# Second self-attention of a two-block transformer kernel: the order of scores, projections, values and row sums

## The chip, the cores and the metric

The kernel runs on one core of one Trainium2 chip. The metric is the device time of one execution in microseconds; lower is better. All arithmetic is in float32.

## What is computed

The input is x of shape 8 x 512 x 256 (batches, rows, width) with a condition vector per batch and a short context. Two blocks follow each other; each has a self-attention, a cross-attention to the context and a feed-forward part, all with residuals. The change lies in the self-attention of the second block. Cut to it, the reference is:

```python
attn_in = _adaln(x, cond, ln1_w, ln1_b, g1_w, g1_b, b1_w, b1_b)   # layer norm, scaled and shifted per batch
q = heads(attn_in @ wq); k, v = heads of (attn_in @ wkv)          # 16 heads of 64
q = _rope(q, sq, cq); k = _rope(k, sk, ck)                        # rotary, on even and odd channels
sim = jnp.einsum('bhnd,bhmd->bhnm', q, k) * 64 ** (-0.5)
a = jax.nn.softmax(sim, axis=-1)
o = jnp.einsum('bhnm,bhmd->bhnd', a, v)
x = unheads(o) @ sa_wo + sa_bo + x
```

The softmax is computed without subtracting a maximum: exponentials of the scores, their products with v, and sums of the exponentials, by which the products are divided at the end.

## The kernel before, in words

The kernel goes through three stages: the first block, the second block's self-attention (the part with the pool "ph4", lines 953 to 1155), and the second block's cross-attention and feed-forward part. In the second, `tc.manual_schedule` is set for PE, DVE, ACT and POOL: each of these engines executes in the order in which the code issues. Only the DMA queue of SP is ordered by the framework.

**The work of a batch.** `batch4(b)` makes the functions for one batch of 512 rows. Heads are handled in NG = 4 groups g of four heads. Keys lie in NT = 4 tiles kt of 128 rows. A step i = 16 b + 4 g + kt is one pair (g, kt), 128 steps in all.

- `score(g, kt)` (line 1003) makes 8 matmuls with 32 contraction rows each, four beside each other in the array, into two tiles of two PSUM banks (`bank_s`, two buffers, so one step fills both). Two exponentials on ACT (L1012) turn them into probabilities p. The pool has six p buffers, two to a step.
- `value(g, kt)` (line 1014) multiplies p with v into one bank O and one bank D, accumulated over kt: 4 matmuls with 64 output rows, two beside each other. At kt = 0 it adds the p of kt 0 and 1 on POOL (L1027, two of them); at kt = 2 it adds the p of kt 2 and 3 to that on DVE (L1031, four). At kt = 3 ACT copies O and D to oT (L1035).
- `sums(g)` (line 1041) is 4 matmuls with ones that add sm over the partitions, into an X bank; ACT copies it (L1047), SP sends it through DRAM back as a dense tile rec.
- `inverse(g)` (line 1057) takes the reciprocal on DVE (L1059), sends it to DRAM, and fetches it back spread over the partitions (rb, L1071, four DMAs).
- `scaled(g)` (line 1074) multiplies oT with rb on POOL (L1077, two).
- `queries(g)` and `keys(g)` (through `turned`, line 983) are a projection into two X banks: even and odd channels, 2 matmuls each. DVE makes four rotary products (L991, L992), POOL adds them up (L994, L995). `values(half, ts)` (line 973) is a projection of the same PE time into two X banks, which ACT copies (L981).
- `out_tiles(qp)` is half of the output projection into one X bank; DVE adds it to x (L453).
- `rows_` is the layer norm of the next batch: on DVE statistics (L183, L184), an add (L174), the normalized rows z (L187, four), with a power on POOL in between (L175); then POOL adds the bias row to x (L437). `turn` transposes z on PE (L416) into two X banks, from which ACT writes hT (L417).

There are two X banks in this stage, used in turn: `bank_x()` gives the one that was taken the longer ago, and its first matmul waits until that bank has been read.

**The slots.** Two steps make a slot; slot m holds the steps 2m and 2m + 1, and a batch begins at slot base = 8 b. `last(slot, fn)` puts a job into the list of a slot. With r = m - base, and b' the next batch, the lists in the middle of the stage are:

| r | jobs in order (before) | kt of the slot |
|---|---|---|
| 0 | values of half 1 (t 0, 1); keys(1); inverse(3) of the batch before | 0, 1 |
| 1 | values of half 1 (t 2, 3); queries(2); scaled(3) of the batch before | 2, 3 |
| 2 | out_tiles(0) of the batch before; keys(2); inverse(0) | 0, 1 |
| 3 | out_tiles(1) of the batch before; queries(3); rows_ of b'; scaled(0) | 2, 3 |
| 4 | keys(3); inverse(1) | 0, 1 |
| 5 | turn of b'; queries(0) of b'; scaled(1) | 2, 3 |
| 6 | values of half 0 of b' (t 0, 1); keys(0) of b'; inverse(2) | 0, 1 |
| 7 | values of half 0 of b' (t 2, 3); queries(1) of b'; scaled(2) | 2, 3 |

The function `slots()` (line 1124) issues, slot by slot: the scores of 2m, the values of 2m - 1, the sums of the group that has just ended (`mid`, in even slots), the scores of 2m + 1, the values of 2m, and then the jobs of the slot. So on PE a slot runs scores, values, (sums), scores, values, projections. The last batch has no next one: its slots 61 and 63 have no job for PE, and slot 62 only the sums.

## Time and profile before

| what | value |
|---|---|
| median of three runs | 2453.35 us (2447.49 to 2454.86) |
| the profiled execution | 2448.82 us, its span 2446.9 us |
| granted TensorE clock, mean | 0.997 |
| stage of the second self-attention (first to last exponential) | 883.5 to 1837 us |
| L1012, exponential | 1022 ns, 256 of them |
| L1031, sum of p on DVE | 1532 ns mean, 128 of them |
| L1027, sum of p on POOL | 2354 ns mean, 64 of them |
| L994 and L995, rotary sums on POOL | 1272 ns mean for the queries, 1480 for the keys |
| L1077, scaling on POOL | 1307 ns mean, 63 of them |
| L991 and L992, rotary product on DVE | 692 and 680 ns |

The profile is one execution. Busy time of an engine is the time in which at least one of its instructions runs. A float32 matmul appears as two records of PE, and records overlap each other, so the start of one group to the start of the next is the better measure of what a group takes on PE. The line of a wait names the instruction on the other engine that came last before the waiting one went on. All PE instructions of matmuls are recorded under the helper's line L109, so groups are told apart by the tiles that they read and write.

### The profile page before, as it was taken

How to read it: one execution, taken by the hardware profiler on the slowest of the kernel's cores; microseconds unless marked ns; L12 is line 12 of the kernel's file. 1: busy time of each engine (PE TensorE's matmuls, PEld its weight loads, DVE VectorE, ACT ScalarE, POOL GpSimd, SP SyncE). 2: the span in 40 equal slices, each digit the busy share in tenths (PEclk: the TensorE clock that was granted, in tenths of full speed). 3: DMA queues.
4: the chain of work that ended last, by engine and by line, in shares of the span. 5: the costliest groups of instructions: out<-in, count | busy, mean ns of one | idle time of the engine just before them, and what ended most of it. 6: DMA issues, size and time to landing. Idle time of an engine off the chain costs nothing.

```text
span 2446.9 us, 28449 instructions
## 1 busy us (share of the span) xinstructions
PE 2408.0 (98%) x10964; PEld 1157.3 (47%) x10964; DVE 1058.9 (43%) x2083; ACT 878.5 (36%) x1118; POOL 858.5 (35%) x538
## 2 busy tenths in 40 slices
PE   9999999999998999999999999999999999999999
PEld 4333443444435643444444444434345555566665
DVE  5544435434434434343434343434334766651210
ACT  4565545545452123333333333333332221222221
POOL 3443222222301026343434343434333444531110
PEclk9999999999999999999999999999999999999999
DMA  5120000000001000000000000000123222210000
GB/s 181 45 93 7 16 20 8 17 11 12 13 11 64 27 1 23 18 19 19 19 18 19 18 19 19 19 18 19 36 61 96 68 67 67 64 55 27 22 18 23
DMA packets 84400, 84.07 MB, mean 34 GB/s; under 512 B 42544, under 2 KB 58784, under 8 KB 84256
## 3 DMA queue, kind: packets, MB, share of 16 engines
q1 hardware_dynamic: 83352, 81.09, 10.6%
q8 instruction: 88, 1.44, 0.2%
q10 hardware_dynamic: 904, 1.07, 0.1%
q14 instruction: 56, 0.46, 0.1%
HBM read 72.09 MB, written 10.04 MB: 34 GB/s over the span
## 4 chain that ended last, share of the span: by engine, by line
PE 92%; DVE 3%; issue 1%; ACT 1%; DMA 1%; POOL 1%; SPq 0%; POOLq 0%; DVEq 0%; ACTq 0%
PE ps_X L109 38%; PE ps_S L109 23%; PE ps_O L109 14%; PE ps_D L109 14%; PE ps_X L416 1%; DVE t L836 1%; DMA rec<-rec 1%; DMA rb<-rec 1%; POOL p L1252 1%; ACT p L574 0%; PE ps_X L554 0%; PE ps_X L596 0%; PE ps_D L416 0%; DVE t L833 0%; ACT hT L417 0%
## 5 line engine op out<-in xcount | busy, mean ns | idle before, releaser
L109 PE MATMUL ps_S<-q,k 32*128 32x512 f32 (+1 forms) x3072 | 429.1, 625 | 7.3 <-ACT p L574 3.1
L1012 ACT ACTIVATE p<-ps_S 128x1024 f32<-128x1024 f32 x256 | 248.1, 1022 | 522.1 <-PE ps_S L109 522.1
L574 ACT ACTIVATE p<-ps_S 128x1024 f32<-128x1024 f32 x256 | 248.2, 1021 | 232.1 <-PE ps_S L109 230.7
L109 PEld LDWEIGHTS ps_S<-q,k 32*128 32x128 f32 (+1 forms) x3072 | 160.5, 184 | 233.1 <-issue 137.5
L991 DVE TENSOR_TENSOR t<-ps_X,rope_c 128x512 f32<-128x512 f32 x126 | 87.2, 692 | 349.9 <-PE ps_X L109 349.9
L1031 DVE TENSOR_TENSOR sm<-sm,p 128x1024 f32<-128x1024 f32 x128 | 190.6, 1532 | 59.2 <-ACT p L1012 59.2
L994 POOL TENSOR_TENSOR q<-t 128x512 f32<-128x512 f32 x32 | 40.8, 1276 | 406.6 <-DVE t L992 406.6
L175 POOL TENSOR_TENSOR rstd<-rstd,mhalf 128x4 f32<-128x4 f32 x49 | 51.0, 1042 | 326.8 <-DVE rstd L174 325.2
L1027 POOL TENSOR_TENSOR sm<-p 128x1024 f32<-128x1024 f32 x64 | 149.3, 2354 | 38.0 <-ACT p L1012 38.0
L109 PE MATMUL ps_X<-hT,w 128*128 128x512 f32 x344 | 160.5, 601 | 1.3 <-ACT hT L417 0.9
L837 POOL TENSOR_TENSOR q<-t,t 128x512 f32<-128x512 f32 x72 | 95.1, 1321 | 176.4 <-DVE t L836 172.4
L109 PE MATMUL ps_O<-p,h 128*32 128x512 f32 x1024 | 139.4, 614 | 1.6 <-ACT oT L587 1.6
L109 PE MATMUL ps_O<-p,v 128*64 128x512 f32 x512 | 138.0, 617 | 0.0
L109 PE MATMUL ps_D<-p,v 128*64 128x512 f32 x512 | 131.6, 592 | 0.0
L453 DVE TENSOR_TENSOR x<-ps_X,x 128x512 f32<-128x512 f32 x27 | 18.7, 692 | 239.4 <-PE ps_X L109 239.4
L109 PE MATMUL ps_X<-hT,w_sa_wq 128*128 128x512 f32 x256 | 115.9, 595 | 3.0 <-ACT hT L417 3.0
L109 PE MATMUL ps_X<-w_sa_wv,hT 128*128 128x512 f32 x256 | 118.0, 604 | 0.0
L109 PE MATMUL ps_X<-w_sa_wo,oT 128*128 128x256 f32 x512 | 114.5, 382 | 0.1
L545 POOL TENSOR_TENSOR var<-var,mhalf 128x32 f32<-128x32 f32 (+1 forms) x17 | 87.3, 5135 | 75.2 <-ACT t L773 41.7
L109 PE MATMUL ps_X<-hT,w_sa_wk 128*128 128x512 f32 x248 | 112.4, 596 | 0.0
L109 PE MATMUL ps_S<-hT,w_ff_w 128*128 128x512 f32 x256 | 111.3, 592 | 0.0
L109 PEld LDWEIGHTS ps_X<-w_sa_wo,oT 128*128 128x128 f32 x512 | 96.0, 190 | 24.2 <-issue 11.4
(282 smaller groups left out, 3537.0 us busy)
## 6 DMA issues: line engine op xcount, KB each, us to landing
rb<-rec SPq DMA_DIRECT2D x128, 128.0 KB
rb<-rec_d SPq DMA_DIRECT2D x124, 128.0 KB
rb<-rec SPq DMA_DIRECT2D x16, 256.0 KB
out_dram<-x SPq DMA_DIRECT2D x15, 256.0 KB
x<-in_x_dram SPq DMA_DIRECT2D x7, 512.0 KB
bc<-modd SPq DMA_DIRECT2D x7, 384.0 KB
gate<-modd SPq DMA_DIRECT2D x16, 128.0 KB
k_d<-q SPq DMA_DIRECT2D x8, 256.0 KB
```

What stands on the lines that cost most here:

```text
L109: nc.tensor.matmul(o, lhsT, rhs, start=start, stop=stop)
L175: nc.gpsimd.tensor_tensor(r[:, :n], r[:, :n], mhalf[:, :n], ALU.pow)
L416: nc.tensor.transpose(ps[:, t * P : (t + 1) * P], z[:, t, k * P : (k + 1) * P], ident)
L545: nc.gpsimd.tensor_tensor(var, var, half, ALU.pow)
L574: nc.scalar.activation(pr[u], pss[u], AF.Exp, scale=HD0 ** -0.5)
L836: nc.vector.tensor_tensor(t2[d], ps[src], sn[src].to_broadcast([64, *shape[1:]]), ALU.mult)
L837: nc.gpsimd.tensor_tensor(dst, t1, t2, ALU.add)
L991: nc.vector.tensor_tensor(c, ps, rope_c, ALU.mult)
L994: nc.gpsimd.tensor_tensor(r[0], ec, os, ALU.subtract)
L1012: nc.scalar.activation(pr, pss[u], AF.Exp, scale=HD1 ** -0.5)
L1027: nc.gpsimd.tensor_tensor(sm, s["p", g, 0, u], s["p", g, 1, u], ALU.add)
L1031: nc.vector.tensor_tensor(s["sm", g, u], s["sm", g, u], s["p", g, t, u], ALU.add)
```

## The change

In each slot the order becomes: the scores of 2m + 1, the first job of the slot, the sums (in even slots), the other jobs, the scores of 2m + 2, the values of 2m and of 2m + 1, and then `inverse`. So a slot runs scores, projection, (sums), projection, scores, values, values on PE. `inverse` leaves the list of jobs for a list of its own, `after`. The sums on POOL and DVE (L1027, L1031) belong to `value`, and so they are issued behind the slot's jobs. The slots begin at m = -1, where the first batch's projections are issued ahead of the first scores, and end with m = 63. The functions of a step and of a job are not changed.

```diff
-        steps, mid = {}, {}
+        steps, mid, after = {}, {}, {}
...
                 n = base + 2 * g + 2
                 mid[n] = lambda g=g, f=sums: f(g)
-                last(n, lambda g=g, f=inverse: f(g))
+                after[n] = [lambda g=g, f=inverse: f(g)]
                 last(n + 1, lambda g=g, f=scaled: f(g))
...
             n = B * NG * NT
-            for i in range(-2, n + 1):
-                if 0 <= i < n:
+            for m in range(-1, n // 2):
+
+                i = 2 * m + 1
+                if i >= 0:
                     todo[i // 16][0](i % 16 // NT, i % NT)
-                if 1 <= i <= n:
-                    todo[(i - 1) // 16][1]((i - 1) % 16 // NT, (i - 1) % NT)
-                if i % 2 == 0 and i // 2 in mid:
-                    mid[i // 2]()
-                if i % 2:
-                    for fn in steps.get(i // 2, []):
-                        fn()
+                jobs = steps.get(m, [])[:]
+                if m in mid:
+                    jobs.insert(1, mid[m])
+                for fn in jobs:
+                    fn()
+                if i + 1 < n:
+                    todo[(i + 1) // 16][0]((i + 1) % 16 // NT, (i + 1) % NT)
+                for k in (i - 1, i):
+                    if k >= 0:
+                        todo[k // 16][1](k % 16 // NT, k % NT)
+                for fn in after.get(m, []):
+                    fn()
                 if i == n - 5:
                     cross_weights()
```

## The prediction

> **What bounds the kernel now.** I read the page's busy times first, then the groups by shape, then the timeline of one batch in the second self-attention (883 to 1841 us).

> ```profile
> span 2446.9 us, 28449 instructions
> PE 2408.0 (98%) x10964; PEld 1157.3 (47%) x10964; DVE 1058.9 (43%) x2083; ACT 878.5 (36%) x1118; POOL 858.5 (35%) x538
> ```

> PE is busy 98%, so whatever adds idle time to PE adds it to the end. In the stage the cycle of eight slots repeats each 119 us almost to the hundredth, so I read prices from start to start of PE groups. Three stretches of the timeline (start, duration, engine, line, output and inputs, count, idle time before):

> ```profile
> 1302.40 3.60 PE L109 MATMUL ps_X<-hT,w_sa_wq 128*128 128x512 f32 x8
> ...
> 1305.00 0.68 DVE L992 TENSOR_TENSOR t<-ps_X,rope_s 128x512 f32<-128x512 f32 x1
> 1305.93 2.00 PE L109 MATMUL ps_S<-q,k 32*128 32x512 f32 x16
> ...
> 1311.23 1.38 DVE L187 TENSOR_SCALAR z<-x,mv,rstd 128x256 f32<-128x256 f32 x4 [1.14 <-POOL rstd L175]
> ...
> 1312.69 2.37 POOL L437 TENSOR_TENSOR x<-x,rows 128x1024 f32<-128x1024 f32 x1 [1.50 <-DVE z L187]
> ```

> The projection ends at 1305.93. Behind it DVE still has half the rotary products and the whole norm of the next batch; z ends at 1312.61, 6.68 us after the projection. Only then can POOL add the bias row.

> ```profile
> 1320.18 1.94 ACT L1012 ACTIVATE p<-ps_S 128x1024 f32<-128x1024 f32 x2 [5.49 <-PE ps_S L109]
> 1320.99 1.03 PE L109 MATMUL ps_D<-p,v 128*64 128x512 f32 x4
> ...
> 1321.31 7.48 DVE L1031 TENSOR_TENSOR sm<-sm,p 128x1024 f32<-128x1024 f32 x4 [1.33 <-ACT p L1012]
> 1321.95 2.21 PE L109 MATMUL ps_S<-q,k 32*128 32x512 f32 x16
> 1322.11 2.25 POOL L994 TENSOR_TENSOR k<-t 128x512 f32<-128x512 f32 x1
> 1324.04 1.94 ACT L1012 ACTIVATE p<-ps_S 128x1024 f32<-128x1024 f32 x2 [1.92 <-PE ps_S L109]
> ...
> 1325.96 1.09 PE L416 MATMUL ps_X<-ident,z 128*128 128x128 f32 x8
> 1326.65 1.45 ACT L417 ACTIVATE hT<-ps_X,b,a 128x512 f32<-128x512 f32 x2 [0.67 <-PE ps_X L416]
> 1327.48 3.70 PE L109 MATMUL ps_X<-hT,w_sa_wq 128*128 128x512 f32 x8 [0.43 <-ACT hT L417]
> ```

> Scores take 1.93 us, but 2.14 (1321.95 to 1324.09) where only one value step stands between two score steps: the exponentials end at 1322.12, after the next scores began. A turn's queries wait 0.43 us for ACT. The four sums (L1031) take 7.48 us because POOL works beside them.

> ```profile
> L1031 DVE TENSOR_TENSOR sm<-sm,p x128: 1209/1224/2298, 899.5 to 1837.8; 128x1024 f32<-128x1024 f32 x128
> ```

> Alone an L1031 takes 1.22 us; beside POOL's rotary sum it takes up to 2.30.

> [...] 1.22 becomes 2.30, near 1.22 plus POOL's 1.27. [...]

> **The change part by part.** I call the slots of a batch r = 0 to 7.

> *Values of two steps together.* A value step alone takes 0.91 + 0.96 = 1.87 us. At the stage's end two stand together already, and the inner groups take 0.86: 0.91 + 0.86 + 0.86 + 0.96 = 3.59 for two instead of 3.74. Gain 63 x 0.15 = 9.5 us.

> *Scores, projections, scores.* 34 score groups follow a value step and take 72.5 us; at 1.93 each they would take 65.6. After the change 3.6 us of values or a projection of 3.5 stand between, so the exponentials (1.94) end in time. Gain 6.9 us. Going from scores straight into a projection never happens in this trace. I take it as costly as from scores into values (both then use all 128 rows): 0. Bounds: free, which removes 0.22 of the scores and 0.10 at the projection's start, 63 x 0.32 = -20 us; or another 0.22 each, +14 us.

> *Sums behind the first projection.* In r = 0, 2, 6 they now split two projections. A 128-row group after a switch costs 0.10 more (3.63 against 3.53), and 0.10 more before one: 0.2 x 21 = 4.2 us. In r = 4 there is one projection, so the sums split nothing: 0 for the switch.

> *The vector queue in r = 3 and 4: the main cost.* Before, the four L1031 of slot r = 3 were queued ahead of that slot's projections. Now value() comes after the jobs, so they stand behind the rotary products and the whole norm, and start at 6.68 us after the projection's end. There they meet POOL's bias row (2.37) and the two scalings (1.28 each), all on SBUF. One after the other: 4 x 1.22 + 2.37 + 2 x 1.28 = 9.8; a contested pair measures 2.3, not 2.5, so I take off 0.2 for each of three: 9.2. They end at 15.9. Behind them in the queue stand the rotary products of keys(3); its even half (1304.39 to 1305.68) takes 1.3, to 17.2. Only then is that X bank free, and sums(1), placed just behind keys(3), takes the next X bank of two, which is that one. With 0.1 for the signal it starts at 17.3. PE is there at 1.93 + 3.59 + 1.93 + 3.63 = 11.1. Stall 6.2 us, in the seven batches with a next one: 43.4 us. Bounds: no contention, 6.68 + 4.9 + 1.4 = 13.0, stall 1.9, 13 us in all; strict alternation, 6.8, 48 us. In the last batch (no norm) the sums end at 1.5 + 4 x 2.3 = 10.7, the rotary half at 12.0, and the stall is 1.0 us.

> *The turn in r = 5.* Before, a value step ran between the scores and the transposes. Now transposes follow at once, and on ACT the copies into hT stand behind two exponentials. From the scores' end: exponentials to 1.9, first copy (half of 1.45 and the latency, 0.8) to 2.7, so the queries start at 2.7 instead of 1.52. Cost 1.2 x 7 = 8.4 us.

> *The end.* In slots 61 and 62 there is no projection left: scores follow scores. At the stage's start such a pair takes 5.94 us instead of 3.86, so 2.1; with sums (1.0) between, 1.1. Cost 3.2 us.

> *Moved at no cost.* inverse() with its reciprocal and five DMAs on SP now comes after the values. In even slots DVE has no L1031, so the reciprocal waits for rec while DVE is empty; behind it stand only the next slot's rotary products, over 8 us off. The rb copies were issued 1321.20 to 1323.58 and used at 1335.21; the sums come 4 to 9 us later than before within the slot, the scaling comes at the end of the next slot's POOL work, so some 10 us remain. If that cover went, scaled() would hold POOL's queue. Probabilities: six buffers are three steps; a step's scores need the buffers two slots' L1031 or L1027 release. POOL's pair (4.7 us, behind 2.5 of rotary sums and 1.5 of DVE) ends 8.7 us after a projection, while the second exponential wants its buffer at 8.5: 0.2 us, hidden by the projection that follows. In r = 0 and 6 the sums want the L1031 at 11.0 us and these end at 10.7: hidden by 0.3 us. If that goes, 15 slots lose some 0.5 us each, 7 us.

> *Sum.* -9.5 - 6.9 + 4.2 + 43.4 + 1.0 + 8.4 + 3.2 = +43.8 us. The profiled execution took 2448.82 us (span 2446.9 and 1.9 around it), giving 2492.6. The median shown is 2453.35, 4.5 us above it, and would give 2497.2. I put the forecast between, at 2494.

> **Rivals.** *Light stall:* POOL's work doesn't slow the sums (its ropes beside PSUM reads show none), so r = 4 loses 1.9 us: 43.8 - 30 = +14, 2464. Against it: a mean of 1532 ns over a median of 1224 (page and row above) means that a quarter or more of the 128 L1031 were slowed to some 2.3 us. *Not slower:* the r = 4 wait doesn't occur at all, sums and rotary half being done by 11.1 us. What is left is 43.8 - 43.4 = +0.4: 2450. It decides from the point where DVE does four L1031 and half a rotation in 4.4 us after z; the rows say 6.2 alone, so the norm would have to be done earlier. For it speaks that the norm has its own inputs, against it the written order. *Worse:* leaving the scores costs 0.22 more and the narrow slots slip as well: 43.8 + 14 + 7, 2515. *The change does nothing:* excluded, since the order of PE is written out by hand and the changed code has the new sequence.

> **How the numbers follow.** Forecast 0.60, with a range of its own from 2478 to 2510 (16 us to either side: the score exit's +14 or most of its -20, and the stall's 48 at the top); light stall 0.18; not slower 0.12; worse 0.10. The range 2462 to 2513 leaves out the not-slower case and half of the worse one, 0.17. About 0.3% (7 us) is what a measurement of this kernel can tell from no change. Faster by more needs the not-slower case and a free exit from the scores: 0.05. Within 0.3%: 0.11. Slower: 0.84.

> **What would show it.** Right: value groups of 0.86 inside a pair; no score group of 2.14; each batch but the last with a PE gap of some 6 us before the sums of r = 4, released by DVE's L992; L1031 in r = 3 starting after L187 and mostly near 2.3; queries after a turn waiting 1.6 instead of 0.43. Wrong: no gap in r = 4, or a projection after scores that takes more or less than 3.63 us.

## The result and the profile after

The changed kernel takes 2475.19 us (median of four runs, 2474.84 to 2479.44) against 2453.04 us before (the three runs above and one more). It is slower by 22 us; the ratio taken over all runs is 1.0098, with a 95% interval of 1.0079 to 1.0118. The forecast was 2494 us with a range of 2462 to 2513. The profiled executions differ by 26.0 us (2474.84 against 2448.82), and all of it lies in the second self-attention: from its first exponential to its last copy of O and D that stage takes 982.1 us instead of 956.2.

The head of the page of the changed kernel:

```profile
span 2472.9 us, 28440 instructions
PE 2404.0 (97%) x10964; PEld 1144.8 (46%) x10964; DVE 1088.0 (44%) x2083; ACT 888.1 (36%) x1118; POOL 959.1 (39%) x538
```

PE has the same instructions and is busy 4 us less, in a span that is 26 us longer. So the matmuls themselves became cheaper, and PE idles more. DVE is busy 29 us longer and POOL 101 us longer with the same work: their instructions now run beside each other more often, and are longer there. The row of L1031 shows it (durations are least, median and greatest, in ns; the median was 1224 before):

```profile
L1031 DVE TENSOR_TENSOR sm<-sm,p x128: 1210/2284/2307, 909.8 to 1863.1; 128x1024 f32<-128x1024 f32 x128
```

The timeline of the changed kernel from r = 3 to r = 5 of one batch (start, duration, engine, line, output and inputs, count, idle time before):

```profile
1313.61 2.00 PE L109 MATMUL ps_S<-q,k 32*128 32x512 f32 x16
...
1318.91 1.38 DVE L187 TENSOR_SCALAR z<-x,mv,rstd 128x256 f32<-128x256 f32 x4 [1.14 <-POOL rstd L175]
1319.12 2.00 PE L109 MATMUL ps_S<-q,k 32*128 32x512 f32 x16
...
1320.21 4.63 DVE L1031 TENSOR_TENSOR sm<-sm,p 128x1024 f32<-128x1024 f32 x4
1320.38 6.68 POOL L437 TENSOR_TENSOR x<-x,rows 128x1024 f32<-128x1024 f32 x1 [1.50 <-DVE z L187]
1321.05 3.70 PE L109 MATMUL ps_X<-hT,w_sa_wk 128*128 128x512 f32 x8
...
1324.75 0.69 DVE L991 TENSOR_TENSOR t<-ps_X,rope_c 128x512 f32<-128x512 f32 x1
...
1326.09 1.06 PE L109 MATMUL ps_X<-sm,ones 128*32 128x512 f32 x8 [1.33 <-DVE t L992]
...
1331.92 4.66 POOL L1027 TENSOR_TENSOR sm<-p 128x1024 f32<-128x1024 f32 x2
...
1334.53 1.09 PE L416 MATMUL ps_X<-ident,z 128*128 128x128 f32 x8
1334.69 1.02 ACT L1012 ACTIVATE p<-ps_S 128x1024 f32<-128x1024 f32 x1 [3.63 <-PE ps_S L109]
1336.62 1.02 ACT L1012 ACTIVATE p<-ps_S 128x1024 f32<-128x1024 f32 x1 [0.91 <-POOL sm L1027]
1337.54 1.44 ACT L417 ACTIVATE hT<-ps_X,b,a 128x512 f32<-128x512 f32 x2
1338.37 1.98 PE L109 MATMUL ps_X<-hT,w_sa_wq 128*128 128x512 f32 x4 [2.75 <-ACT hT L417]
```

Three things are to be seen. First, the sums of r = 4 wait 1.33 us for DVE's rotary product, as forecast in kind, but not 6.2: the four L1031 ran through in 4.63 us, and it was POOL's bias row that took longer (6.68 us instead of 2.37). Second, that put POOL's queue late: L1027 comes late, so the second exponential of r = 5 waits for its buffer until 1336.62, and behind it on ACT the copies into hT. The queries of the turn wait 2.75 us. Third, in some batches the matmuls behind that gap run at half the clock. The two stretches below are the queries of one batch and of another (columns: length, busy time of each engine, then the granted clock, DMA share, GB/s):

```profile
1465.00:1468.00 3.00, 3.00 (x5) 1.12 (x4) 0.00 (x0) 0.00 (x0) 0.00 (x0) 0.50 0.00 0
1338.00:1342.00 4.00, 3.63 (x9) 1.44 (x9) 1.29 (x2) 0.98 (x2) 0.00 (x0) 1.00 0.00 0
```

From starts of groups on PE, the whole difference adds up, next to the forecast's terms:

| term | forecast, us | measured, us |
|---|---|---|
| values in pairs | -9.5 | -9.5 (0.91, 0.86, 0.86, 0.96 in every slot) |
| scores no longer late | -6.9 | -6.9 (all 63 behind values take 1.93) |
| scores straight into a projection | 0 | 0 (1.93; the projection 3.54 where another follows it, 3.63 where not) |
| projections split by the sums | +4.2 | +4.0 |
| wait before the sums of r = 4 | +43.4 + 1.0 | +8.4 in six batches, +3.8 in the first, 0 in the last |
| turn | +8.4 | +15.4 (2.3 in six batches, 1.5 in the first) |
| end of the stage | +3.2 | +3.0 |
| half clock | not foreseen | +6.4 behind three turns, +0.9 in the first batch's sums |
| sum | +43.8 | +25.5 (the stage: +25.9) |

The first batch is another case: in its r = 4 another job stands first in the list, so its sums come ahead of keys(3), straight behind the scores, and wait for L1031 itself: 2.7 us before the first two matmuls and 1.1 before the other two. The 1.1 is read from the kernels below in which the clock stays full there (2.12 us for these sums instead of 1.00); here they take 2.99.

### The profile page after: what moved, and what is told of

Same layout as the page of the kernel before. It is cut to its first block, busy times and chain, and to the rows that moved or that the text cites. A ratio compares the mean times of both kernels' runs of the same rounds, so it can differ in the third digit from the quotient of the medians.

```text
span 2472.9 us, 28440 instructions
## 1 busy us (share of the span) xinstructions
PE 2404.0 (97%) x10964; PEld 1144.8 (46%) x10964; DVE 1088.0 (44%) x2083; ACT 888.1 (36%) x1118; POOL 959.1 (39%) x538
## 4 chain that ended last, share of the span: by engine, by line
PE 85%; DVE 4%; POOL 4%; issue 4%; ACT 2%; DMA 1%; SPq 0%; POOLq 0%; DVEq 0%; ACTq 0%
PE ps_X L109 37%; PE ps_S L109 20%; PE ps_D L109 13%; PE ps_O L109 13%; POOL sm L1027 1%; PE ps_X L416 1%; DVE t L836 1%; DMA rb<-rec 1%; POOL p L1259 1%; ACT p L574 0%; DMA rec<-rec 0%; ACT p L1012 0%; PE ps_X L554 0%; DVE st L183 0%; SPq L1252 0%
## 5 line engine op out<-in xcount | busy, mean ns | idle before, releaser
L109 PE MATMUL ps_S<-q,k 32*128 32x512 f32 (+1 forms) x3072 | 422.8, 622 | 9.3 <-DVE k L558 3.6
L1012 ACT ACTIVATE p<-ps_S 128x1024 f32<-128x1024 f32 x256 | 252.2, 1023 | 492.7 <-PE ps_S L109 471.3
L109 PEld LDWEIGHTS ps_S<-q,k 32*128 32x128 f32 (+1 forms) x3072 | 142.2, 183 | 248.0 <-issue 178.6
L991 DVE TENSOR_TENSOR t<-ps_X,rope_c 128x512 f32<-128x512 f32 x126 | 87.0, 691 | 374.4 <-PE ps_X L109 374.3
L1031 DVE TENSOR_TENSOR sm<-sm,p 128x1024 f32<-128x1024 f32 x128 | 222.7, 1799 | 2.0 <-ACT p L1012 2.0
L994 POOL TENSOR_TENSOR q<-t 128x512 f32<-128x512 f32 x32 | 59.7, 1866 | 306.1 <-DVE t L992 306.1
L175 POOL TENSOR_TENSOR rstd<-rstd,mhalf 128x4 f32<-128x4 f32 x49 | 51.0, 1041 | 327.0 <-DVE rstd L174 325.4
L109 PE MATMUL ps_X<-hT,w 128*128 128x512 f32 x344 | 160.5, 601 | 1.3 <-ACT hT L417 0.9
L1027 POOL TENSOR_TENSOR sm<-p 128x1024 f32<-128x1024 f32 x64 | 149.1, 2353 | 3.4 <-ACT p L1012 3.4
L109 PE MATMUL ps_X<-hT,w_sa_wq 128*128 128x512 f32 x256 | 122.3, 623 | 18.4 <-ACT hT L417 18.4
L109 PE MATMUL ps_O<-p,h 128*32 128x512 f32 x1024 | 137.8, 608 | 1.6 <-ACT oT L587 1.6
L109 PE MATMUL ps_O<-p,v 128*64 128x512 f32 x512 | 134.8, 605 | 0.0
L109 PE MATMUL ps_D<-p,v 128*64 128x512 f32 x512 | 131.6, 592 | 0.0
L1077 POOL TENSOR_TENSOR oT<-oT,rb 128x512 f32<-128x512 f32 x63 | 123.5, 1978 | 18.7 <-DMA rb<-rec_d 18.7
L109 PE MATMUL ps_X<-w_sa_wv,hT 128*128 128x512 f32 x256 | 118.0, 604 | 0.0
L994 POOL TENSOR_TENSOR k<-t 128x512 f32<-128x512 f32 x32 | 40.8, 1274 | 192.3 <-DVE t L992 185.0
L109 PE MATMUL ps_X<-hT,w_sa_wk 128*128 128x512 f32 x248 | 114.7, 605 | 0.0
L109 PE MATMUL ps_X<-w_sa_wo,oT 128*128 128x256 f32 x512 | 114.5, 382 | 0.1
```

The lines of the kernel that those rows point to most:

```text
L109: nc.tensor.matmul(o, lhsT, rhs, start=start, stop=stop)
L175: nc.gpsimd.tensor_tensor(r[:, :n], r[:, :n], mhalf[:, :n], ALU.pow)
L991: nc.vector.tensor_tensor(c, ps, rope_c, ALU.mult)
L994: nc.gpsimd.tensor_tensor(r[0], ec, os, ALU.subtract)
L1012: nc.scalar.activation(pr, pss[u], AF.Exp, scale=HD1 ** -0.5)
L1027: nc.gpsimd.tensor_tensor(sm, s["p", g, 0, u], s["p", g, 1, u], ALU.add)
```

## The experiments

The theory after this reading: gains on PE of 16 us are real; the loss is three waits, and they hang together: the norm ahead of L1031 delays the sums and POOL; late POOL delays the turn; a long idle time of PE is followed by half clock. The rival for the first is that of the forecast, contention of L1031 with the rotary sums and scalings themselves; for the turn, that it waits for two exponentials only; for the clock, that the slow matmuls have another cause than idle time. All times below are medians; before took 2450.1 to 2450.4 us beside them.

**The norm one slot earlier.** It is issued ahead of its slot's projections.

```diff
-                last(base - 5, rows_)
+                if b > 1:
+                    early[base - 6] = rows_
+                else:
+                    last(base - 5, rows_)
...
+                if m in early:
+                    early[m]()
                 jobs = steps.get(m, [])[:]
```

> The changed kernel, with the norm of batches 2 to 7 issued one slot earlier (r = 2, ahead of that slot's projections), so that in r = 3 the four L1031 stand behind the rotary products alone. Theory A (the norm ahead of L1031 is what makes the sums of r = 4 wait, and POOL's late bias row is what makes the exponential behind L1027, and with it the turn, late): the 1.4 us before the sums of r = 4 vanish in six batches (-8.4 us), the turn's transposes and wait shrink from 3.84 to about 2.7 us in those six (-6.8 us), and PE idle of 2.75 us is gone, so with it the half-clock stretches behind the turn (-6.4 us): 2475 - 21 = 2454 us. Rival B (the turn waits for two exponentials only, whatever POOL does, as I predicted, and the surplus of 1.1 us is something else): only the 8.4 us go, 2467 us. Rival C (the wait of r = 4 comes from contention of L1031 with the rotary sums and the scalings and not from the norm): no gain at r = 4, about 2475 us.

Measured: 2458.33 us (2453.76 to 2463.73), ratio to before 1.0032 (1.0020 to 1.0044). In one of the six batches:

```profile
1313.37 7.86 DVE L1031 TENSOR_TENSOR sm<-sm,p 128x1024 f32<-128x1024 f32 x4
...
1323.06 1.06 PE L109 MATMUL ps_X<-sm,ones 128*32 128x512 f32 x8
...
1331.50 1.09 PE L416 MATMUL ps_X<-ident,z 128*128 128x128 f32 x8
1331.66 1.94 ACT L1012 ACTIVATE p<-ps_S 128x1024 f32<-128x1024 f32 x2 [3.63 <-PE ps_S L109]
...
1334.32 3.70 PE L109 MATMUL ps_X<-hT,w_sa_wq 128*128 128x512 f32 x8 [1.73 <-ACT hT L417]
```

The wait of r = 4 is gone in all six batches, though L1031 take 7.86 us for four there, beside rotary sums and scalings: that alone costs nothing here, since L1031 start early enough to be done in time. From the start of the transposes to the queries it is 2.82 us in the six batches instead of 3.84, and the second exponential no longer waits for POOL. So rivals B and C fall. Half-clock stretches remained behind two of the seven turns, for 3.3 us together, which is most of the 4 us over the expectation. Its runs spread by 10 us, and their granted clocks go with the time: 0.997 in the fastest, 0.992 in the slowest.

**The turn ahead of the scores.** It is issued first in slot r = 5.

```diff
-                last(base - 3, turn)
+                ahead[base - 3] = turn
...
                 i = 2 * m + 1
+                if m in ahead:
+                    ahead[m]()
```

> The changed kernel, with turn (the transposes and the copies into hT) issued directly behind the values of r = 4, ahead of the scores of r = 5; nothing else moved. Theory A (the copies into hT wait on ACT behind the exponentials of the scores just ahead): the copies now run beside the scores, the queries find hT ready, the transposes take about 1.2 us instead of 3.84 (3.0 in the first batch): 6 x 2.6 + 1.8 = -17.5 us, and without the idle of 2.75 us the half-clock stretches behind the turn go too (-6.4 us): 2475 - 24 = 2451 us. Rival (the copies wait for something that the turn's place does not change, such as the bias row or z): the wait moves ahead of the scores and the time stays at 2470 to 2475 us.

Measured: 2451.26 us, ratio 1.0002 (0.9993 to 1.0010): the 24 us of the expectation. The queries follow the scores without a gap, on PE in r = 5:

```profile
1325.66 2.00 PE L109 MATMUL ps_S<-q,k 32*128 32x512 f32 x16
1327.59 3.70 PE L109 MATMUL ps_X<-hT,w_sa_wq 128*128 128x512 f32 x8
```

The wait of r = 4 stayed at 1.41 us in six batches, as it should. No half-clock stretch is left in the stage. The place of the turn behind the scores was the largest single loss (15.4 us, and 6.4 of half clock behind it).

**Every turn's transposes twice.**

```diff
-            for t in range(NT):
+            for t in [*range(NT)] * (2 if twice else 1):
...
-                s["hT"] = transposed(nk, s["z"], b, a1, b1, 1)
+                s["hT"] = transposed(nk, s["z"], b, a1, b1, 1, twice=True)
```

> The changed kernel with every turn's eight transposes made twice, into the same banks; the second time overwrites the same values. This is extra PE work in a stretch in which PE waits for ACT anyway. Theory A (after the turn TensorE's clock halves in some batches because PE idled 2.75 us): PE now idles some 1.7 us there, the granted clock stays full, the queries take 3.63 us in all batches, and 6.4 us go: 2469 us. The wait of the queries for hT itself is unchanged. Rival (the slow matmuls behind the turn have another cause than the idle time, or the idle time is not what decides): the slow stretches remain, 2475 us, or with 1.1 us for each turn's extra transposes on the path, 2483 us.

Measured: 2475.82 us, 1.0107 (1.0090 to 1.0124): a miss of the time. The extra transposes cost nothing, since ACT is waited for anyway (3.85 us as before), but PE still idled 1.88 us, and two of the seven turns were still followed by half clock, for 1.7 us each. The stage was 3.6 us shorter in the profile, the whole execution 0.4. So this alone neither confirmed nor refuted idle time as the cause. A gap of 1.88 us stays just below the 1.91 us from which half clock always came here, and above the 1.72 us up to which it never did (the counts, by the part of a gap within one window, are in the last section).

**The bias row in four, and in two.**

```diff
-                add_row(b, row("sabo"))
+                for t in range(NT):
+                    nc.gpsimd.tensor_tensor(xs[b][:, t, :], xs[b][:, t, :], row("sabo"), ALU.add)
```

> The changed kernel with POOL's bias row in the norm's job cut from one instruction of 128 x 1024 into four of 128 x 256; the same sums. In the changed kernel the four L1031 beside it take 4.63 us, as if alone, and the bias row 6.68 us instead of 2.37. Theory A ([...]POOL's long one was held off by four L1031 that follow without a gap, because DVE came first): with four short ones POOL gets turns between L1031, as the rotary sums do (7.86 us for four), so L1031 end up to 3 us later, the wait before the sums of r = 4 grows from 1.4 to 3 to 4.7 us, POOL's queue is done earlier and the turn waits less: 2475 + 6 x 2.5 - 6 x 1 = 2484 us. Rival (POOL is held off by back-to-back L1031 whatever the size of its instruction): L1031 stay at 4.6 us and the time at 2475 us.

Measured: 2508.45 us, 1.0236 (1.0219 to 1.0253). The four L1031 took 7.83 us, and the wait before the sums of r = 4 was 5.4 us, with a half-clock stretch of 6.83 us behind each of these waits. Direction and course of theory A hold; the size was missed: the wait grew by 4.0 us where 2.5 was taken, and the half clock was not in the sum. The time from the transposes to the queries fell from 3.84 to 2.82 us, as expected, though PE now also comes there later. The second form keeps the broadcast operand and only halves the instruction:

```diff
-                add_row(b, row("sabo"))
+                for h in range(2):
+                    xh = xs[b][:, 2 * h : 2 * h + 2, :]
+                    nc.gpsimd.tensor_tensor(xh, xh, row("sabo")[:, None, :].to_broadcast([P, 2, D]), ALU.add)
```

> The changed kernel with POOL's bias row cut into two instructions of 128 x 512 that keep its broadcast row operand. This tells what let four L1031 through beside the one long instruction, 4.6 us for four, and not beside four short ones. Theory A (the length or number decides: a 128 x 512 of POOL gets its turn between L1031, as the rotary sums do): L1031 take about 7.8 us for four and the wait before the sums of r = 4 grows from 1.4 to 3 to 5.5 us: 2495 to 2508 us. Rival (the broadcast operand of the bias row decides): L1031 stay near 4.6 us for as long as a bias row stands beside them, and the time at 2470 to 2480 us.

Measured: 2504.22 us, 1.0229 (1.0212 to 1.0247). In its r = 3 (its lines are two further down, so L1033 is L1031, L1079 is L1077 and L994 is L992):

```profile
1332.07 2.33 DVE L187 TENSOR_SCALAR z<-x,mv,rstd 128x256 f32<-128x256 f32 x4 [1.13 <-POOL rstd L175]
...
1332.88 1.36 POOL L970 TENSOR_TENSOR x<-x,rows 128x512 f32<-128x512 f32 x1 [0.85 <-DVE z L187]
...
1334.32 7.83 DVE L1033 TENSOR_TENSOR sm<-sm,p 128x1024 f32<-128x1024 f32 x4
1334.48 2.18 POOL L970 TENSOR_TENSOR x<-x,rows 128x512 f32<-128x512 f32 x1 [0.23 <-DVE z L187]
1336.62 4.45 POOL L1079 TENSOR_TENSOR oT<-oT,rb 128x512 f32<-128x512 f32 x2
...
1343.41 1.93 PE L109 MATMUL ps_X<-sm,ones 128*32 128x512 f32 x8 [5.50 <-DVE t L994]
```

The second half of the bias row started 0.16 us after the first L1031 and took 2.18 us, done before the second L1031 was; the whole row, which started 0.17 us after, took 6.68 us and ended 2.2 us behind all four. With the halves the wait is 5.5 us, 4.2 more than in the changed kernel. L1031 give 3.2 of these (7.83 us instead of 4.63); the other 0.95 comes from z, which takes 2.33 us instead of 1.38 beside the first half of the bias row. That term was not in the forecast, and its 9.2 us for L1031 were too many, so its 6.2 is met in part by errors that cancel. But its chain, from slowed L1031 to the rotary product and the bank, is what happened with the bias row in halves; in the changed kernel it failed at the assumption that the 128 x 1024 bias row would lengthen L1031 too.

**Both moves together, and a version with the rest mended.**

> The changed kernel with both earlier edits: the norm of batches 2 to 7 one slot earlier, and the turn directly behind the values of r = 4. Theory A (the wait before the sums of r = 4 and the turn's wait are two separate losses, and what is left over the kernel before is only the first batch's wait of 2.7 us, the split projections, 4.2 us, and the end, 3.0 us): 2451.3 - 6 x 1.4 = 2443 us, 7 us faster than before. Rival (the two share one cause, so that with the turn moved the norm's move brings nothing more): 2451 us.

Measured: 2444.11 us, 0.9971 (0.9960 to 0.9982). The two losses are separate: the wait of the turn is gone in all seven batches, that of r = 4 in all but the first. The next kernel adds three things to this one; its edit against the changed kernel is this, with the calls of `early` and `ahead` as above:

```diff
-                last(base - 5, rows_)
-                last(base - 3, turn)
+                early[base - (6 if b > 1 else 7)] = rows_
+                ahead[base - 3] = turn
...
-                    jobs.insert(1, mid[m])
+                    jobs.append(mid[m])
...
+                ks = [k for k in (i - 1, i) if k >= 0]
+                if m >= n // 2 - 3:
+                    k = ks.pop(0)
+                    todo[k // 16][1](k % 16 // NT, k % NT)
                 if i + 1 < n:
                     todo[(i + 1) // 16][0]((i + 1) % 16 // NT, (i + 1) % NT)
-                for k in (i - 1, i):
-                    if k >= 0:
-                        todo[k // 16][1](k % 16 // NT, k % NT)
+                for k in ks:
+                    todo[k // 16][1](k % 16 // NT, k % NT)
```

> As the one before, and also: the first batch's norm early as well (r = 1), the sums behind all projections of a slot (so that no projection is split, and in the first batch they no longer come ahead of keys(3)), and in the last three slots one value step between the two score steps. Theory A: -4.2 us for the 21 split projections, -4.7 us for the first batch's wait with its slow sums, -2.4 us at the end: 2443 - 11 = 2432 us, 18 us faster than before. Rival (sums behind the last projection wait for DVE's rotary half of that projection, because they take the bank that it reads): the 4.2 us come back as waits, 2436 us or more.

Measured: 2430.80 us, 0.9917 (0.9903 to 0.9931), 20 us faster than before and 44 us faster than the changed kernel. In the stage no group on PE is late by more than 0.3 us, but for the first two scores. Its page and its r = 5 (lines are one further down):

```profile
PE 2391.9 (98%) x10964; PEld 1145.0 (47%) x10964; DVE 1112.1 (46%) x2083; ACT 885.5 (36%) x1118; POOL 954.6 (39%) x538
```

```profile
1315.63 1.09 PE L416 MATMUL ps_X<-ident,z 128*128 128x128 f32 x8
...
1316.33 1.45 ACT L417 ACTIVATE hT<-ps_X,b,a 128x512 f32<-128x512 f32 x2 [2.24 <-PE ps_X L416]
1316.66 2.00 PE L109 MATMUL ps_S<-q,k 32*128 32x512 f32 x16
1318.59 3.70 PE L109 MATMUL ps_X<-hT,w_sa_wq 128*128 128x512 f32 x8
```

The copies into hT run beside the scores. DVE and POOL are as busy as in the changed kernel: that their instructions lengthen each other costs PE next to nothing here, where nothing on PE waits for their last instruction.

**The values one by one again.**

```diff
+                ks = [k for k in (i - 1, i) if k >= 0]
+                if ks:
+                    k = ks.pop(0)
+                    todo[k // 16][1](k % 16 // NT, k % NT)
                 if i + 1 < n:
                     todo[(i + 1) // 16][0]((i + 1) % 16 // NT, (i + 1) % NT)
-                for k in (i - 1, i):
-                    if k >= 0:
-                        todo[k // 16][1](k % 16 // NT, k % NT)
+                for k in ks:
+                    todo[k // 16][1](k % 16 // NT, k % NT)
```

> The changed kernel with one value step on either side of the second scores: scores, projections, values, scores, values. This undoes the pairing of the values alone; the projections, sums and norm stay where the change put them. Theory A (a pair saves 0.15 us in a slot, and a lone value step behind scores lets the next scores wait 0.21 us for the exponentials): 63 x 0.36 = +22.7 us, less 2.4 us at the end and some 2.5 us of the wait at r = 4, which PE reaches later: 2475 + 18 = 2493 us. Rival (what the pairing saves on PE is lost in what follows it, so that it is worth nothing): 2475 us.

Measured: 2492.95 us, 1.0178 (1.0162 to 1.0194), 17.8 us over the changed kernel where 18 were expected. The second scores of this slot are late again:

```profile
1370.54 2.00 PE L109 MATMUL ps_S<-q,k 32*128 32x512 f32 x16
1372.47 1.08 PE L109 MATMUL ps_O<-p,v 128*64 128x512 f32 x4
1373.38 1.03 PE L109 MATMUL ps_D<-p,v 128*64 128x512 f32 x4
1374.34 2.21 PE L109 MATMUL ps_S<-q,k 32*128 32x512 f32 x16
1376.48 3.70 PE L109 MATMUL ps_X<-w_sa_wv,hT 128*128 128x512 f32 x8
```

1.93 us from the first scores to the values, 2.14 from the second to the projection. The pairing's two gains are real: by starts in the whole stage, the values take 9.5 us more and the scores some 15. That the sum came out to 0.2 us is in part luck: half clock cost 2.7 us more than in the changed kernel and the turn 2.3 less, and neither was expected.

**The sums behind all projections.**

```diff
-                    jobs.insert(1, mid[m])
+                    jobs.append(mid[m])
```

> The changed kernel with the sums behind all projections of their slot instead of behind the first. Theory A (a switch to the 32-column sums and back between two projections costs 0.1 us at each side): -4.2 us, and in the first batch, where the sums of slot 4 now come behind keys(3), about -4 us: 2467 us. Rival (the switch costs nothing, or the sums then wait for the bank): 2471 us or more.

Measured: 2477.56 us, 1.0109 (1.0094 to 1.0125): a miss. On PE the split is gone, as expected (the keys behind a projection take 3.53, not 3.63), and the sums don't wait for the bank, so theory and rival were both right on those. What ate it: half-clock stretches followed all seven turns instead of three, 15.1 us instead of 6.4, and the first batch's turn waited 4.1 us instead of 1.5. With the split and the first batch's sums (4.0 and 3.3 us less) that makes +4.0, as the stage shows (986.1 us against 982.1). The gaps of six turns are as long as before, 2.73 to 2.74 us; a shift of a few microseconds in time changed which of them half clock follows. That the gap is the cause was tried directly, with this kernel's transposes made three times:

> The kernel with the sums behind all projections, with every turn's transposes made three times into the same banks (the same values again), so that PE idles some 0.8 us at a turn instead of 2.74; the copies into hT, which wait for ACT, should start as before. In the profiles so far TensorE's clock halved after a gap whenever 1.91 us or more of PE idle time fell within one window of 3.413 us[...], and never when the share was under 1.7 us. Theory A (it is the idle time within a window that halves the clock, and this is what ate the gain of the sums' move, 15.1 us behind the seven turns of that kernel): in six batches no half-clock stretch follows a turn, at least 12 of the 15.1 us go, and the time is 2477.6 - 13 = 2464 us; the first batch, with a longer wait, may keep its own. Rival (the gap only moves the stretch, or the sums' move costs for another reason): 2474 to 2478 us.

Measured: 2465.86 us, 1.0067 (1.0050 to 1.0084), 11.7 us less by adding work. The turn without and with it, first in the kernel with the sums last, then with three times the transposes:

```profile
1335.99 1.09 PE L416 MATMUL ps_X<-ident,z 128*128 128x128 f32 x8
1339.83 5.40 PE L109 MATMUL ps_X<-hT,w_sa_wq 128*128 128x512 f32 x8 [2.74 <-ACT hT L417]
```

```profile
1207.40 2.84 PE L416 MATMUL ps_X<-ident,z 128*128 128x128 f32 x24
1211.27 3.70 PE L109 MATMUL ps_X<-hT,w_sa_wq 128*128 128x512 f32 x8 [1.03 <-ACT hT L417]
```

The queries start 3.84 and 3.87 us after the transposes, so they start no earlier, but PE idles 1.0 us instead of 2.7 and they take 3.7 instead of 5.4 us. In six batches no half clock follows a turn; in the first, whose gap stays at 2.77 us, it does. So here PE's idle time is what half clock followed, and it is what ate the gain.

## Why the prediction was right or wrong

The direction and the range were right, the size was not: +44 was forecast, +22 came. By its steps:

- *What bounds the kernel*, right: every term of the difference is PE time, and the table closes to 0.4 us. One reading was loose: 119 us is the mean of the stage's batches, while a batch with an output projection takes 123.7.
- *Values in pairs* and *scores, projections, scores*, right to 0.1 us by the profile, and confirmed in kind by the run that undid the pairing. That scores into a projection cost no more than scores into values, a guess with wide bounds, was right too. (The 0.22 us in those bounds are what scores take beyond 16 records at the pace of the trace before, four in 0.43 us: 1.93 against some 1.72. That leaving or entering the scores is what costs them was my estimate.)
- *Sums behind the first projection*, right: 4.0 us; undone, they went, though the time didn't show it.
- *The vector queue in r = 3 and 4*, the step that failed, by its main term. Place, order and waiting instruction were right, and moving the norm removed the wait. But "one after the other", an estimate from one pair (L1031 up to 2.30 us, near 1.22 and 1.27 together), was wrong for the bias row: L1031 took 1.22 us each and ended 4.63 us after the first began, not 9.2, so the wait was 1.4 us, close to the light bound of 1.9 that stood beside it. Cut into two, the bias row gives nearly what was forecast (5.5 us), 0.95 of it by z, which the forecast did not have. In the first batch the sums stand ahead of keys(3), which the forecast missed too (3.8 us there).
- *The turn*, right in its cause, low by 1.1 us in six batches: the two exponentials were counted, but not that the second one would wait for L1027. The text had priced POOL's pair in even slots as hidden "by the projection that follows"; what follows in r = 5 is the turn, which has no such cover. That is the same queue of POOL, late by the bias row: with the norm earlier the surplus went.
- *The end*, right (3.0). *Moved at no cost*: the reciprocal and its DMAs cost nothing, right.
- *Missing*: the clock. Added idle time on PE was priced at its own length, and 7.3 us more came on top.

The errors have opposite signs: the wait was 32 us too high, the turn and the clock together 14 us too low. That the result lies well inside the range is therefore in part luck: with the wait alone put right, the forecast would have been 2462 us, the range's lower end. The likeliest case was the wrong one; the nearest was the rival called light stall (2464 us), for another reason than the one it gave: POOL's work did slow L1031 (2.28 us in the median after), but the bias row beside those four did not (1.22 us each), and itself took 6.68 us.

## What to carry to other kernels

When a written order is changed, list what each in-order queue then does between the moved instruction and its reader, on every engine that shares a buffer with it; here the gain was in the order on PE, and all of the loss but 3 us at the stage's end came from three jobs (norm, turn, sums) left at places that had suited the old order. With these moved along, and the last three slots mended, the change made the kernel 20 us faster than before instead of 22 us slower. And a gap of 2 to 3 us on TensorE was here often not paid by its length alone: behind three of the six turn gaps of 2.74 to 2.76 us, half clock cost 6.4 us more together.

## What the runs showed of the hardware that had not been expected

**DVE's sums beside POOL's instructions.** Beside four L1031 in a row, POOL instructions of 128 x 512 took 2.1 to 2.3 us instead of 1.27, and the four L1031 7.8 to 7.9 us instead of 4.6, as if the two engines took turns. One of 128 x 1024 that started 0.17 us after the first L1031 took 6.68 us beside four that took 4.63, as if all four went first. A POOL instruction of 128 x 1024 that had started first kept its time before the change, and L1031 was the longer one (L1027 2.37 us; L1031 some 1.93 us instead of 1.22 in eight places). Not every DVE instruction is lengthened: the rotary products L991, which read PSUM, took 691 to 692 ns in the 16 places before the change where L1027 or L1077 ran beside them, against 690 to 693 in all. Why the two engines lengthen each other was not shown. Whether length or something else in the long instruction decides was not tried further than that halving it changed the outcome and that the broadcast operand alone is not it.
